# Other deadlines for two closing quarters of the last pair, and one reload split over two queues

## The chip, the cores and the metric

The kernel runs on one core of one Trainium2 chip. The metric is device time in microseconds (us): the median of three runs of the whole kernel. One further execution was taken with the hardware profiler. All durations below that belong to single instructions are from that one execution.

The engines are named as in the profile: PE is TensorE, DVE is VectorE, ACT is ScalarE, POOL is GpSimd, SP is SyncE. SP and ACT issue the DMA transfers of this kernel. Each of them works through its own list of instructions in order, so an issue that has to wait holds up everything behind it in that list.

## The reference

What is computed is one conditioned transformer-like block on `x` of shape (2, 2048, 512) in float32:

```python
emb = jnp.dot(jax.nn.silu(t), ada_w) + ada_b
shift_msa, scale_msa, gate_msa, shift_mlp, scale_mlp, gate_mlp = jnp.split(emb, 6, axis=-1)
norm = _ln(x) * (1.0 + scale_msa[:, None]) + shift_msa[:, None]
h = jax.nn.gelu(jnp.dot(norm, ssm_w1) + ssm_b1, approximate=False)
ssm_out = jnp.dot(h, ssm_w2) + ssm_b2
x = x + gate_msa[:, None] * ssm_out
norm2 = _ln(x) * (1.0 + scale_mlp[:, None]) + shift_mlp[:, None]
hf = jax.nn.gelu(jnp.dot(norm2, ff_w1) + ff_b1, approximate=True)
ff_out = jnp.dot(hf, ff_w2) + ff_b2
x = x + gate_mlp[:, None] * ff_out
```

Both weights of the first half are 512 x 512, `ff_w1` is 512 x 1024 and `ff_w2` 1024 x 512. The change touches only the last line, for the last tokens.

## The kernel before

**Tiling.** The 4096 tokens are cut into 8 blocks of 512. The first half of the function runs block by block. The second half, the feed-forward, runs on pairs of blocks: `ff` goes through four pairs, s = 0 to 3, first `up(s)`, then `down(s)`. "The last pair" is s = 3, and `closing` or `last` in the code means this pair.

**Fewer products.** All matrix products are done by a two-level scheme that replaces eight block products by seven, with sums of operands before and sums of results after. `down(s)` has seven outer products in the order P1, P2, P3, P6, P5, P7, P4 (`DOWN`, L939), and each of them seven inner ones, called leaves, in the order P1, P5, P6, P2, P7, P3, P4 (`CARRIED`, L447). Two outer products run interleaved: a leaf of one, then a leaf of the next. A leaf leaves its result in a PSUM bank, and DVE or ACT carries it into `summed`, four rows of results `r0` to `r3` in the tile `rows`. Operand sums run on DVE or POOL, as the planner decides.

**The quarters of a pair's result.** The result of a pair has four quarters: block 0 or 1 (`blk`) by the left or right half of the features (`d`). It stands with features on the partitions and tokens along them and has to be turned before it is added to the residual `x1`.

- In the last pair the two quarters with d = 0 go through DRAM, by `quarter_out` (L1065). The first, `blk` 0, is complete after outer product P2 (row `r0`); the second, `blk` 1, after outer product P5 (row `r3`). `quarter_out` transposes 32 x 32 blocks by two DVE instructions (L1073) into a band of the tile `far`, stores the four slices of the band to a DRAM buffer (`back`) on SP and ACT in turn, loads the buffer back into the same row (`rows<-back`, one load of 512 KB on SP), adds it in two halves (h = 0, 1) to the residual, and stores each half to the output, the first from SP and the second from ACT. The residual of the first quarter stands in the tile `far`, that of the second in `near`. So `out_dram<-far` are the first quarter's closing stores and `out_dram<-near` the second's.
- The two quarters with d = 1 are scaled and summed by DVE (`scaled_add`, L1045), then turned by PE with an identity matrix (`turned_by_pe`, L1183, matmuls on line 306), added to the residual in the tile `hidden` and stored in eight pieces of 128 KB, `out_dram<-hidden`. The turn of a leaf is put into PE's list two leaves later. Outer product P7 feeds one of these quarters by wide adds (128 x 512), P4 the other by narrow ones (128 x 256). P5 feeds `r3` by narrow scaled adds. The text below calls the add that follows a turn a `hidden` add.

**What sets the order.** The order of work on every engine is laid out when the program is built. Each operation is entered into `Plan` with an assumed cost. `order` (L89) gives each matmul a due time, at which it would start if PE ran without a gap, t being the end of that; it gives each closing store the due time t + 3000 ns (L101). From these it counts back a latest start (`late`) for every operation:

```python
late = min(late, ops[s].late - (1 + op.care) * (self.HOP + min(op.lat.values()) + op.size / self.RATE))
```

HOP is 70 ns and RATE 370 bytes per ns; `care` is 0.45 for all of the feed-forward (L1381 sets it last). The assumed latency is 2000 ns for a DMA, n/0.96 + 155 ns for a DVE add of n columns, n/0.96 + 205 for a scaled add, and 705 for a transpose. `simulate` (L113) then plays the program. On each engine it takes, of the operations that are ready, the one with the smallest `late` (`rank`, L141); it waits for one that is not ready only if that one is due to start before the ready one would end, has a smaller `late` than it, and can begin at least 150 ns before that end. PE's list keeps the order of the program. The result is a fixed list for each engine, which the chip works through in order.

Of the kernel before, what the change touches and what calls it, by code (L numbers as in the profile page):

```python
# [20 lines left out]
class Plan:  # L21
# [67 lines left out]
    def order(self):  # L89
        ops = self.ops  # L90
        for op in ops:
            if op.engs == "p":
                op.deps = {d for d in op.deps if ops[d].engs != "p"}
            for d in op.deps:
                ops[d].succ.append(op.n)
        t, due = 0.0, {}
        for op in ops:
            if op.engs == "p":
                due[op.n] = t
                t += op.cost["p"]  # L100
        due.update((n, t + 3000.0) for n in self.closing)  # L101
        for _ in range(2):
            for op in reversed(ops):
                late = due.get(op.n, 1e9)
                for s in op.succ:
                    late = min(late, ops[s].late - (1 + op.care) * (self.HOP + min(op.lat.values()) + op.size / self.RATE))
                op.late = late - op.sooner
            self.simulate()
            wait = ops[self.anchor].start - due[self.anchor]
            due = {n: t + wait for n, t in due.items()}  # L110
        return sorted(ops, key=lambda op: (op.start, op.n))
# [89 lines left out]
def kernel(  # L201
# [28 lines left out]
    M = P // G  # L230
# [6 lines left out]
    plan = Plan(nc)  # L237
# [6 lines left out]
    def cols(ap):  # L244
        n = 1
        for d in ap.shape[1:]:
            n *= d
        return n
# [4 lines left out]
    def tt(e, o, a, b, f):  # L253
        n, ps = cols(o), in_psum(a, b)
        cost = {"v": n / 0.96 + 70, "g": 2.12 * n + 145}
        plan.add(
            e,
            lambda E: E.tensor_tensor(o, a, b, f),  # L258
            [o],
            [a, b],  # L260
            cost,
            {"v": cost["v"] + 85, "g": cost["g"] + 45},
            "g" if ps else "vg",
        )
# [5 lines left out]
    def act(o, a, func, bias=0.0, scale=1.0):  # L270
        n = cols(o)
        ptrs = [p for p in (bias, scale) if not isinstance(p, float)]
        cost = n / 1.4 + (155, 215, 340)[len(ptrs)] + (30 if func == AF.Gelu_apprx_tanh else 0)
        plan.add(
            "a",
            lambda E: E.activation(o, a, func, bias=bias, scale=scale),  # L276
            [o],
            [a] + ptrs,
            {"a": cost},
            {"a": cost + 90},  # L280
        )
# [21 lines left out]
    def turn_by_pe(o, a, identity, start, stop):  # L303
        plan.add(
            "p",
            lambda E: E.matmul(o, a, identity, start=start, stop=stop, is_transpose=True, skip_group_check=True),  # L306
            [o],
            [a, identity],
            {"p": 120.0},
            {"p": 290.0},  # L310
        )

    def dma(o, a, q="s", lead=0.0, lat=2000.0, sooner=0.0):
        size = max(cols(o.unsqueeze(0)), 1) * 4
        outs = [o] if o.tensor.name in scratch else []
        ins = [a] if a.tensor.name in scratch else []
        lead = lead or (0.0 if ins or not outs or size <= plan.LITTLE else 25000.0)
        plan.add(q, lambda E: E.dma_start(out=o, in_=a), outs, ins, {q: plan.ISSUE}, {q: lat}, size=size, lead=lead)
        plan.ops[-1].sooner = sooner
# [24 lines left out]
    def kb(t, at, n):  # L344
        return t[:, at * 256 : (at + n) * 256]

    def cut(t, form, **sizes):
        return t.rearrange(form, **sizes)
# [6 lines left out]
    for n in range(8):  # L355
        t = psum.tile([P, 2 * HT], F32, tag=f"bank{n}", name=f"bank{n}")
# [699 lines left out]
    def columns(s, d, e, blk):  # L1056
        k, b = 2 * d + e, (2 * s + blk) // PER_B
        return gb5[:, k, b : b + 1], mods[5][:, k, b : b + 1]

    def rest_in(s, d, blk, x):  # L1060
        half = slice(d * D // 2, (d + 1) * D // 2)
        dma(x, x1_d[2 * s + blk][:, :, half])
        return x, out_blk[2 * s + blk][:, :, half]

    def quarter_out(s, d, blk, r, scaled=False):  # L1065
        done = summed[:, r]
        n = quarters[0] % 2
        for e in range(0 if scaled else 2):
            act(done[:, e], done[:, e], AF.Identity, *columns(s, d, e, blk))
        band = cut(bands[n], "p (a c e r) -> p e c a r", a=M, c=C, e=2)  # L1070
        for e in range(2):
            o, a = band[:, e], cut(done[:, e], "p (c a q) -> p c a q", c=C, a=M)
            plan.add("v", lambda E, o=o, a=a: E.transpose(o, a), [o], [a], {"v": 636}, {"v": 705})  # L1073
        closing = s + 1 == NBLK // 2
        queue = lambda f: "sa"[f % 2] if closing else "s"
        far_t = back_d[s][d][blk]
        for f in range(M):
            dma(far_t[:, f].rearrange("(a q) r -> q a r", a=M), cut(bands[n][f * G : (f + 1) * G], "p (a r) -> p a r", a=M), queue(f))
        flat = done.rearrange("p e t -> p (e t)")
        dma(flat, far_t.rearrange("p f r -> p (f r)"))  # L1080
        x, to = rest_in(s, d, blk, rest[n])
        for h in range(2):
            c = slice(2 * h, 2 * h + 2)
            o = cut(x[:, c], "p c (e f r) -> p (c e) f r", e=2, f=M)
            a = cut(flat, "p (f c e r) -> p c e f r", f=M, c=C, e=2)[:, c].rearrange("p c e f r -> p (c e) f r")
            tt("v" if closing else "vg", o, a, o, ALU.add)
            if closing:
                dma(to[:, c], x[:, c], queue(h))
                plan.closing.append(plan.ops[-1].n)
        if not closing:  # L1090
            dma(to, x)
        quarters[0] += 1

    def down(s):
# [22 lines left out]
        def leaf(n, f):  # L1117
# [23 lines left out]
            elif p == "P2":  # L1141
                add(r0, r1 if new else r0)
                if f == "P4":
                    quarter_out(s, 0, 0, 0)
# [5 lines left out]
            elif p == "P5":  # L1150
                if last:
                    scaled_add(r3, t, columns(s, 0, e, 1)[1])
                add(r2, r1 if new else r2)
                if full and last:
                    act(part[:, 1:3], part[:, 1:3], AF.Identity, *columns(s, 1, e, 0))
                elif full:
                    tt("vg", r3, r3, r2, ALU.add)
                if f == "P4":
                    quarter_out(s, 0, 1, 3, last)
            elif p == "P7":  # L1160
                both, wide = part[:, 1:3], t.unsqueeze(1).to_broadcast([P, 2, HT])
                if last:
                    scaled_add(both, wide, columns(s, 1, e, 0)[1])
                else:
                    tt("v", both, wide, both, ALU.add)
                if last:
                    turned_by_pe(1, 2, f, quad)
                elif f == "P4":
                    quarter_out(s, 1, 1, 2)
            elif not last:  # L1170
                add(r1, r1)
                if f == "P4":
                    quarter_out(s, 1, 0, 1)
            else:
                scaled_add(r1, t, columns(s, 1, e, 0)[1])
                turned_by_pe(0, 1, f, quad)
# [6 lines left out]
    def turned_by_pe(blk, r, f, quad):  # L1183
        got = tail[blk]
        if not got:
            got["x"], got["out"] = rest_in(NBLK // 2 - 1, 1, blk, cut(kb(hidden_r, 8 * blk, 4), "p (c d) -> p c d", c=C))

        def turned_back():
            e, h = int(quad[0]) - 1, int(quad[1]) - 1
            bank = cut(banks[TURNED_AT[blk][h]], "p (c e d) -> p c e d", c=2, e=2)  # L1190
            for c in range(2):
                col = slice((2 * h + c) * P, (2 * h + c + 1) * P)
                turn_by_pe(bank[:, c, e], summed[:, r, e, col], ident, c == 0 and h not in got, c == 1)
            got[h] = True
            c, d = slice(2 * h, 2 * h + 2), slice(e * P, (e + 1) * P)
            x = got["x"][:, c, d]
            tt("v", x, bank[:, :, e], x, ALU.add)
            dma(got["out"][:, c, d], x, "sa"[e])
            plan.closing.append(plan.ops[-1].n)

        n = leaves_read[0] = leaves_read[0] + 1
        if f in ("P7", "P2", "P3", "P4"):
            waiting.append((n, turned_back))
        done = blk == 0 and f == "P4"
        while waiting and (done or waiting[0][0] + 2 <= n):
            waiting.pop(0)[1]()
# [240 lines left out]
```

## Time and profile before

| | us |
|---|---|
| median of three runs (lowest, highest) | 564.51 (564.48, 564.86) |
| the profiled execution | 564.89 |
| its span, first to last instruction | 563.1 |
| PE busy in the span | 552.2 (98%) |
| DVE busy in the span | 479.8 (85%) |
| POOL busy in the span | 384.7 (68%) |
| ACT busy in the span | 282.6 (50%) |

The span is 1.8 us shorter than the profiled execution's time; these lie outside its first and last instruction. The profiled execution was 0.38 us longer than the median.

How to read the lines below. In the chain that ended last, a line is start, length, and what held up the end during it. In the order of time, a line is start, length from first to last instruction of the line, engine, source line, operation, what it writes and reads, the shape, how many instructions are merged, and in brackets the idle time just before it with what ended it. Lengths of neighbours on one engine can overlap a little. `SPq` and `ACTq` are the lists that issue DMA; such a line shows when the issue happened, not when the data moved. In the table by stretches, each engine has its busy time and the count of instructions, and the last three numbers are the granted PE clock, the mean busy share of the 16 DMA engines, and GB/s moved. A line of waits is who waited on whom, total us, times, and the longest.

### The profile page before, as it was taken

To read this page: it belongs to the slowest core of one execution; us is meant where nothing else is said; L and a number is where in the kernel's file an instruction comes from. 1 tells how busy PE (TensorE), PEld (TensorE's weight loads), DVE (VectorE), ACT (ScalarE), POOL (GpSimd) and SP (SyncE) were. 2 spreads that over 40 slices of the span, in tenths; PEclk is the share of its full clock that TensorE was granted. 3 is DMA by queue.
4 is the path that set the end of the run, shared out by engine and by line. 5 is a ranking of instruction groups with operands and counts; after the bars stand their busy time and mean duration, and the time that the engine had idled before them with its cause. 6 is when DMAs were issued, how large, how long until landed. Compare 5 with 4: busy or idle time off the path is not lost.

```text
span 563.1 us, 8745 instructions
## 1 busy us (share of the span) xinstructions
PE 552.2 (98%) x2809; PEld 481.2 (85%) x2809; DVE 479.8 (85%) x848; ACT 282.6 (50%) x523; POOL 384.7 (68%) x475
## 2 busy tenths in 40 slices
PE   7999999999999999999999999999999999999994
PEld 4888889888898988888878888888888888888883
DVE  5696878888778588899999996799988989998986
ACT  3473867674877855566205337414337315345230
POOL 2887747979945399984746778676767666547590
PEclk9999999999999999999999999999999999999998
DMA  8963899989399978994202899602998603974317
GB/s 310 399 228 79 234 349 312 330 258 274 100 288 318 303 289 257 334 281 166 75 2 50 286 331 313 210 17 63 306 321 298 183 33 104 309 252 154 108 38 224
DMA packets 66034, 123.68 MB, mean 220 GB/s; under 512 B 5653, under 2 KB 33221, under 8 KB 64453
## 3 DMA queue, kind: packets, MB, share of 16 engines
q1 hardware_dynamic: 63696, 121.53, 66.0%
q10 hardware_dynamic: 2292, 1.60, 1.0%
q8 instruction: 22, 0.36, 0.3%
q14 instruction: 24, 0.19, 0.1%
HBM read 77.89 MB, written 44.18 MB: 217 GB/s over the span
## 4 chain that ended last, share of the span: by engine, by line
PE 89%; DVE 6%; DMA 3%; issue 0%; POOL 0%; DVEq 0%; SPq 0%; ACTq 0%; POOLq 0%
PE bank L296 88%; DVE rows L258 2%; DMA fw<-in_L_cond_ada_w_dram 1%; DVE near L258 1%; DVE far L258 1%; DMA rows<-back 1%; DVE fw L258 1%; DMA back<-far 1%; PE bank L306 0%; DMA fw<-in_L_cond_ada_b_dram 0%; DVE far L1073 0%; DVE hidden L258 0%; POOL far L258 0%; POOL fw L258 0%; POOL rows L258 0%
## 5 line engine op out<-in xcount | busy, mean ns | idle before, releaser
L296 PE MATMUL bank<-turned,ring 128*128 128x256 f32 x896 | 210.2, 380 | 0.2 <-DVE turned L660 0.2
L296 PEld LDWEIGHTS bank<-turned,ring 128*128 128x128 f32 x896 | 167.9, 190 | 23.2 <-DVE turned L660 0.4
L258 DVE TENSOR_TENSOR hidden<-bank,hidden 128x512 f32<-128x512 f32 (+2 forms) x178 | 126.5, 740 | 23.4 <-PE bank L296 19.6
L296 PE MATMUL bank<-near,hidden 128*128 128x256 f32 (+1 forms) x470 | 95.1, 350 | 0.0
L296 PEld LDWEIGHTS bank<-near,hidden 128*128 128x128 f32 x470 | 82.2, 190 | 9.4 <-POOL near L258 0.3
L296 PE MATMUL bank<-far,fw 128*128 128x256 f32 (+1 forms) x354 | 86.0, 374 | 0.2
L258 POOL TENSOR_TENSOR turned<-turned 128x512 f32<-128x512 f32 (+1 forms) x62 | 70.4, 1146 | 20.6 <-DVE turned L258 9.1
L296 PE MATMUL bank<-ring 128*128 128x256 f32 x336 | 82.4, 379 | 0.0
L258 DVE TENSOR_TENSOR rows<-bank,rows 128x256 f32<-128x256 f32 (+1 forms) x142 | 66.2, 479 | 15.4 <-PE bank L296 11.4
L296 PEld LDWEIGHTS bank<-far,fw 128*128 128x128 f32 x354 | 66.5, 190 | 9.6 <-issue 0.5
L296 PEld LDWEIGHTS bank<-ring 128*128 128x128 f32 x336 | 63.7, 190 | 9.1 <-issue 0.5
L285 ACT COPY bank<-bank 128x512 f32<-128x512 f32 (+2 forms) x84 | 37.7, 449 | 62.1 <-PE bank L296 55.8
L276 ACT ACTIVATE hidden<-hidden,cols 128x512 f32<-128x512 f32 (+1 forms) x66 | 44.8, 710 | 43.0 <-DVE hidden L258 42.9
L258 POOL TENSOR_TENSOR hidden<-hidden 128x128 f32<-128x128 f32 (+2 forms) x45 | 43.5, 976 | 25.8 <-DVE hidden L258 13.0
L296 PE MATMUL bank<-near,fw 128*128 128x256 f32 (+1 forms) x246 | 60.7, 377 | 0.0
L296 PE MATMUL bank<-hidden,fw 128*128 128x256 f32 (+1 forms) x216 | 53.3, 376 | 0.5 <-DVE rows L258 0.4
L296 PEld LDWEIGHTS bank<-near,fw 128*128 128x128 f32 x246 | 46.1, 190 | 6.4 <-DVE rows L258 0.2
L276 ACT ACTIVATE turned<-turned,mod,mod 128x512 f32<-128x512 f32 x56 | 42.3, 807 | 9.2 <-DMA turned<-turned 8.5
L296 PEld LDWEIGHTS bank<-hidden,fw 128*128 128x128 f32 x216 | 40.3, 190 | 6.5 <-DVE rows L258 0.8
L276 ACT ACTIVATE rows<-rows,gb,mod 128x512 f32<-128x512 f32 (+1 forms) x34 | 26.7, 787 | 36.9 <-DVE rows L258 25.0
L258 POOL TENSOR_TENSOR ring<-turned,ring 128x256 f32<-128x256 f32 x42 | 30.6, 740 | 20.7 <-PE bank L296 17.0
L258 POOL TENSOR_TENSOR fw<-fw 128x256 f32<-128x256 f32 (+1 forms) x38 | 35.5, 945 | 11.4 <-DMA fw_parts<-fw 3.9
(123 smaller groups left out, 735.4 us busy)
## 6 DMA issues: line engine op xcount, KB each, us to landing
ring<-fw_parts SPq DMA_DIRECT2D x28, 512.0 KB, 5.0
turned<-far SPq DMA_DIRECT2D x52, 256.0 KB, 4.4
ring<-fw_parts SPq DMA_DIRECT2D x28, 384.0 KB, 5.4
turned<-turned SPq DMA_DIRECT2D x32, 256.0 KB, 5.6
rows<-back SPq DMA_DIRECT2D x14, 512.0 KB, 5.5
back<-far SPq DMA_DIRECT2D x52, 128.0 KB, 3.0
fw_parts<-fw SPq DMA_DIRECT2D x21, 256.0 KB, 4.8
fw<-in_L_cond_ada_w_dram SPq DMA_DIRECT2D x5, 1024.0 KB
```

Source lines behind the costliest of these rows:

```text
L258: lambda E: E.tensor_tensor(o, a, b, f),
L276: lambda E: E.activation(o, a, func, bias=bias, scale=scale),
L285: plan.add("a", lambda E: E.copy(o, a), [o], [a], {"a": cost}, {"a": cost + 60})
L296: lambda E: E.matmul(o, lhsT, rhs, start=start, stop=stop, skip_group_check=True, **kw),
```

## The change

The list of closing stores now holds a due time for each store. Before, each was due at t + 3000 ns. After, the first quarter's two closing stores are due at t - 4000, the second quarter's at t - 1000, and the eight stores of the turned quarters at t + 3000 as before. And for the second quarter alone, the reload of 512 KB on SP becomes two of 256 KB, the first on SP and the second on ACT. Each brings the columns that one of the two adds needs: in each of the four slots of 256 columns, the first or the last 128.

```diff
-        due.update((n, t + 3000.0) for n in self.closing)
+        due.update((n, t + late) for n, late in self.closing)
...
         flat = done.rearrange("p e t -> p (e t)")
-        dma(flat, far_t.rearrange("p f r -> p (f r)"))
+        by_slots = lambda t, h: cut(t, "p (f h r) -> p h f r", f=M, h=2)[:, h]
+        for h in range(2 if closing and blk else 0):
+            dma(by_slots(flat, h), far_t.rearrange("p f (h r) -> p h f r", h=2)[:, h], queue(h))
+        if not closing or not blk:
+            dma(flat, far_t.rearrange("p f r -> p (f r)"))
...
                 dma(to[:, c], x[:, c], queue(h))
-                plan.closing.append(plan.ops[-1].n)
+                plan.closing.append((plan.ops[-1].n, -1000.0 if blk else -4000.0))
...
             dma(got["out"][:, c, d], x, "sa"[e])
-            plan.closing.append(plan.ops[-1].n)
+            plan.closing.append((plan.ops[-1].n, 3000.0))
```

## The prediction

> **What bounds the kernel now.** I read the chain of work that ended last first, then the order of time of each queue and engine in the last 20 us, then the DMA share by stretches.
>
> ```profile
> 461.13 85.76 PE bank L296 x396
> ...
> 547.59 0.70 DVE far L1073
> ...
> 548.72 3.63 DMA back<-far
> 552.36 0.67 DVE far L258
> ...
> 553.64 4.22 DMA rows<-back
> ...
> 557.88 0.69 DVE near L258
> 558.57 0.60 DVEq L1442
> ```
>
> TensorE sets the time up to 546.9 us, unbroken since 461.13. From there the end is one thing: the second quarter of the last pair (blk 1, rows `r3`), which is transposed, stored to DRAM, loaded back, added and stored. The kernel loses 16 us between TensorE's release and the span's end at 563.1. The change touches only this tail, so its worth is read there.
>
> ```profile
> 548.32 0.78 SPq L318 DMA_DIRECT2D back<-far  x2
> 549.15 0.72 SPq L318 DMA_DIRECT2D out_dram<-hidden  x1
> 553.05 0.40 SPq L318 DMA_DIRECT2D out_dram<-far  x1
> 553.64 0.34 SPq L318 DMA_DIRECT2D rows<-back  x1
> ...
> 558.60 0.37 SPq L318 DMA_DIRECT2D out_dram<-near  x1
> ```
> ```profile
> 554.05 0.40 ACTq L318 DMA_DIRECT2D out_dram<-far  x1
> ...
> 559.20 0.38 ACTq L318 DMA_DIRECT2D out_dram<-near  x1
> ```
> ```profile
> SPq L318 <- DVE rows L1049: 4.0, 2, 3.5
> ```
>
> The last rows are SP's queue, ACT's queue, and SP's waits between 549 and 553.2. SP stands 3.5 us in one wait, on VectorE, ahead of the first quarter's store (`out_dram<-far`); the load `rows<-back` is queued behind it. The first quarter was loaded back long before (534.07, below): only its add was late.
>
> ```profile
> 542.94 3.00 DVE L1049 SCALAR_TENSOR_TENSOR rows<-bank,mod,rows 128x256 f32<-128x256 f32 x5
> 545.86 0.70 DVE L1073 STREAM_TRANSPOSE far<-rows 128x512 f32<-128x512 f32 x1
> 546.92 0.75 DVE L1049 SCALAR_TENSOR_TENSOR rows<-bank,mod,rows 128x512 f32<-128x512 f32 x1 [0.36 <-PE bank L296]
> 547.59 0.70 DVE L1073 STREAM_TRANSPOSE far<-rows 128x512 f32<-128x512 f32 x1
> ...
> 548.52 0.41 DVE L258 TENSOR_TENSOR hidden<-bank,hidden 128x256 f32<-128x256 f32 x1
> 548.86 0.75 DVE L1049 SCALAR_TENSOR_TENSOR rows<-bank,mod,rows 128x512 f32<-128x512 f32 x1
> 549.53 0.41 DVE L258 TENSOR_TENSOR hidden<-bank,hidden 128x256 f32<-128x256 f32 x1
> ...
> 552.34 0.68 DVE L258 TENSOR_TENSOR far<-rows,far 128x512 f32<-128x512 f32 x1
> 552.94 0.48 DVE L1049 SCALAR_TENSOR_TENSOR rows<-bank,mod,rows 128x256 f32<-128x256 f32 x1
> 553.33 0.68 DVE L258 TENSOR_TENSOR far<-rows,far 128x512 f32<-128x512 f32 x1
> 553.93 0.48 DVE L1049 SCALAR_TENSOR_TENSOR rows<-bank,mod,rows 128x256 f32<-128x256 f32 x1
> 554.33 0.75 DVE L258 TENSOR_TENSOR hidden<-bank,hidden 128x256 f32<-128x256 f32 x2
> ...
> 556.33 0.76 DVE L258 TENSOR_TENSOR hidden<-bank,hidden 128x256 f32<-128x256 f32 x2 [0.20 <-PE bank L306]
> 557.88 1.29 DVE L258 TENSOR_TENSOR near<-rows,near 128x512 f32<-128x512 f32 x2 [0.79 <-DMA rows<-back]
> ```
>
> This is VectorE in order of time. Starts follow each other more closely than durations say: 0.40 us for a narrow scaled add (553.93 to 554.33), 0.67 for a wide one (548.86 to 549.53), 0.62 for a transpose, 0.60 for a first-quarter add (`far`), 0.33 for a `hidden` add. The second transpose (547.59) stands behind a wide add that waited 0.36 us for TensorE. At the end VectorE waits 0.79 us for the load.
>
> ```profile
> 549.00:552.50 3.50, 3.50 (x19) 3.06 (x19) 3.12 (x7) 0.81 (x1) 0.63 (x1) 1.00 0.89 220
> 552.50:554.00 1.50, 1.50 (x11) 1.27 (x10) 1.50 (x4) 0.00 (x0) 0.00 (x0) 1.00 0.08 22
> 554.00:556.00 2.00, 1.30 (x8) 0.91 (x7) 2.00 (x7) 0.00 (x0) 0.00 (x0) 1.00 1.04 208
> 556.00:561.50 5.50, 0.51 (x4) 0.27 (x3) 2.18 (x5) 0.00 (x0) 0.00 (x0) 0.67 1.07 349
> ```
>
> The last two numbers are DMA share and GB/s. The engines idle from 552.5 to 554 and are then full from 556 to 561.5, moving 349 GB/s x 5.5 us = 1.92 MB. So the end is also a matter of bytes: the first quarter's stores (512 KB) and the load (512 KB), both held back, fall on top of the closing stores.
>
> **The ranks.** The planner lists each engine's operations by a rank, the latest start that still meets a deadline, counted back from the end of the matmuls t with 1.45 times its own costs (`care` 0.45). These are its numbers, not times of the chip; I use them only for order. A closing add stands 1.45 x 0.758 = 1.10 us before its store, so the first quarter's adds move from t+1.90 to t-5.10 and the second quarter's from t+1.90 to t-2.10. Back from there: a whole load 5.06, a half load 4.03, the stores 3.51, a transpose 1.12. The transposes go from t-7.80 to t-10.77. The wide add of 546.92 has t-8.03 (its turn on TensorE is due at t-6.86), the wide one before the first transpose, in the group of five, t-9.13. Old ranks reproduce the trace: -9.13, transpose, -8.03, transpose.
>
> **Part 1, the second quarter leaves earlier.** The two transposes now rank ahead of both wide adds. Nothing is added or removed. The group of five at 542.94 holds, by the view of its source line,
>
> ```profile
> L1049 DVE SCALAR_TENSOR_TENSOR rows<-bank,mod,rows x5: 476/744/751, 542.9 to 545.2; 128x512 f32<-128x512 f32 x3, 128x256 f32<-128x256 f32 x2
> ```
>
> three wide and two narrow; by the order of the leaves the last is wide. One narrow, two wide and one narrow remain ahead: 542.94 + 0.40 + 0.67 + 0.67 + 0.40 = 545.08, and two transposes of 0.62 end at 546.32, against 548.29. The four `back` stores then go at 546.35 instead of 548.32: **-1.97 us**. Late in return are the two wide adds: 546.32 and 546.99. Behind the first waits TensorE's turn:
>
> ```profile
> 547.37 0.35 PEld L306 LDWEIGHTS bank<-far,rows 128*128 128x128 f32 x2
> ```
>
> It ends at 547.07 and the weights load at 547.37, a cover of 0.30 us; if that goes, each further VectorE operation ahead costs 0.4 to 0.7 us on TensorE. I take nothing. Upstream, the accumulations and ACT operations into `r3` rank about 3 us earlier too and may trade places with operand sums on VectorE and GpSimd; TensorE had no gap there. I take 0, bounds -0.2 and +1.3 (two first-quarter adds' worth).
>
> **Part 2, the first quarter's adds move forward.** At t-5.10 they pass both early `hidden` adds (t+2.29) and three narrow or wide adds (t-4.58 to t-3.48), not those due earlier. In the places of 548.52 and 549.53 they run at about 548.0 and 549.53. The `out_dram<-far` stores leave SP at about 548.6 instead of 553.05 and ACT at about 550.2 instead of 554.05: 512 KB into a stretch before 552.5-554, where the share is 0.08. Two `hidden` adds of 0.33 go to the freed 1.20 us after 552.3. VectorE's total is unchanged; I take 0.15 us off the last `hidden` add (bounds 0 and 0.2, its own wait).
>
> **Part 3, the load.** The first quarter shows the interval from store to load on a free SP, and the page the median landing of all such loads:
>
> ```profile
> 530.19 0.80 SPq L318 DMA_DIRECT2D back<-far  x2
> 534.07 0.34 SPq L318 DMA_DIRECT2D rows<-back  x1
> ```
> ```profile
> rows<-back SPq DMA_DIRECT2D x14, 512.0 KB, 5.5
> ```
>
> 3.88 us, so at best 546.35 + 3.88 = 550.2. If a `hidden` store stands ahead on SP or ACT, the load waits for that add: after 550.13, two narrow and one wide add (1.47) and two `hidden` adds give 552.3. I take 552.3, nearest to how SP stands now. With 4.22 us (553.64 to 557.85) it lands at 556.5, before VectorE's last `hidden` add ends (557.09, now 556.95). The wait of 0.79 goes; late next is VectorE itself. Both halves cost one more issue (0.4 us, ACT free then) and moves runs an eighth as long (512 bytes, 4 KB before). The eight 128 KB `hidden` stores have such runs and share the stretch of 349 GB/s. Bounds for the split: -0.60 (the first add under the second half) and +1.3 (4.22 against the 5.5 us of the page's row below); both bounds count only past 556.95, until when VectorE covers the load, so I take 0. The Trainium skill ("DMA: Bandwidth & Descriptors", section "Issuing engines are not separate DMA queues") speaks against the split: transfers started by two engines share the same 16 DMA engines and interleave, and only issue time is saved. By that rule the halves land together and the split is worth 0 even when the load is late; no run here shows it yet.
>
> **Sum.** The last store leaves at 559.20 - 0.79 - 0.15 = 558.26: -0.94. It took 3.9 us to land. The 128 KB `back` stores of the first quarter took
>
> ```profile
> DMA to landing us min/median/max: 2.7/2.7/2.7
> ```
>
> so 256 KB alone needs 2.7 + 128 KB / 349 GB/s = 3.1 us; 0.8 was queueing. From 556 on there remain 768 + 512 = 1280 KB instead of 1.92 MB, 1.8 us less of full DMA, which is enough to clear most of it. Between -0.94 (3.9 stays) and -1.74 (3.1) I take **-1.5**, since the bytes left bind less than the issue. Profiled execution: span 563.1, 564.89 us in all; 564.89 - 1.5 = 563.4. That run lies 0.38 above the median, so from the median 564.51: **563.0 us**. 0.2% is 1.13 us, about what a measurement of this kernel can tell from no change.
>
> **Rivals.**
> *VectorE only* (0.17). The wait goes, but the last store still lands in 3.9 us since `hidden` and `near` stores now follow each other more closely. For it: six of eight `hidden` stores are issued after 554.7. Against: 640 KB less after 556. 564.51 - 0.94 = 563.6.
> *The load stays late* (0.15). The loads are queued on SP and ACT behind `hidden` stores whose adds run after 553, or the ranks change little: landing at 557.5 or later. With both halves at 557.5, 1.29 us of adds end at 558.8: 564.1, and up to 564.5 if nothing moves. By the skill's rule above it is this; if the first half came 0.73 us (256 KB / 349 GB/s) earlier, it would be 563.5.
> *Slower* (0.08). The earlier ranks put transposes and first-quarter adds ahead of the scaled adds that TensorE's turns wait for. It decides as soon as over 0.30 us more stands ahead of the add ending at 547.07. Two first-quarter adds (1.20) and a transpose (0.62) there make 1.8 - 0.3 = 1.5 us stall; all of the tail follows, and the gain at the end, bound by TensorE then, is lost: 564.51 + 1.3 to 1.5 = 565.9.
>
> **How the numbers follow.** The forecast has 0.60 and is the case of faster (562.2 to 563.38); same is the next two, 0.17 and 0.15: 0.32; slower 0.08. The range reaches from 562.2 (-2.3: the load at 550.2 and the second quarter's adds ahead of the last `hidden` adds) to 564.7 (nothing moves, or a small stall).
>
> **What would show it.** Right: the transposes follow each other directly and the `back` stores go near 546.4; `out_dram<-far` leaves SP before 550; two 256 KB loads issue by 552.5; no wait for DMA ahead of the `near` adds; the share in 552.5 to 554 rises and the full stretch after 556 ends before 560.5; span near 561.6. Wrong: a new TensorE wait on VectorE at the turns of 547 to 549, a gap in the matmuls between 461 and 547, a load still issued after 553, or last stores that take 3.9 us again.

## The result, and the profile after

| | before | after |
|---|---|---|
| median of nine runs (us) | 564.72 | 563.16 |
| lowest to highest | 564.48 to 565.1 | 563.06 to 563.47 |
| profiled execution, span | 564.89, 563.1 | 563.11, 561.3 |

The ratio after to before is 0.9973 with a 95% interval of 0.9963 to 0.9983: 1.56 us less. The profiled spans differ by 1.8 us. Of this 0.16 arose before the tail: the narrow add of VectorE that waits for TensorE before the group of five starts at 542.60 before and at 542.44 after. About 1.64 us come from the stretch that the change touches, the tail from this add to the end of the span: 20.5 us before, 18.9 after.

First SP's list, then ACT's, of the changed kernel in order of time. A line is start, length, and what is issued.

```profile
546.02 0.78 SPq L318 DMA_DIRECT2D back<-far  x2
548.63 0.41 SPq L318 DMA_DIRECT2D out_dram<-hidden  x1
550.41 0.40 SPq L318 DMA_DIRECT2D out_dram<-far  x1
550.98 0.53 SPq L318 DMA_DIRECT2D rows<-back  x1
...
557.56 0.37 SPq L318 DMA_DIRECT2D out_dram<-near  x1
```
```profile
551.01 0.40 ACTq L318 DMA_DIRECT2D out_dram<-far  x1
551.59 0.60 ACTq L318 DMA_DIRECT2D rows<-back  x1
...
558.16 0.38 ACTq L318 DMA_DIRECT2D out_dram<-near  x1
```

The `back` stores go 2.30 us sooner than at 548.32, the reload 2.66 us sooner on SP, the first quarter's first store 2.64 us sooner, and the last store 1.04 us sooner. From the last store to the end of the span it took 561.3 - 558.16 = 3.1 us, where it took 3.9.

VectorE of the changed kernel, in order of time:

```profile
543.29 0.71 DVE L1073 STREAM_TRANSPOSE far<-rows 128x512 f32<-128x512 f32 x1
544.23 1.14 DVE L1049 SCALAR_TENSOR_TENSOR rows<-bank,mod,rows 128x256 f32<-128x256 f32 x2 [0.23 <-PE bank L296]
545.29 0.70 DVE L1073 STREAM_TRANSPOSE far<-rows 128x512 f32<-128x512 f32 x1
545.92 2.03 DVE L1049 SCALAR_TENSOR_TENSOR rows<-bank,mod,rows 128x512 f32<-128x512 f32 x3
...
549.37 0.41 DVE L258 TENSOR_TENSOR hidden<-bank,hidden 128x256 f32<-128x256 f32 x1
549.70 1.28 DVE L258 TENSOR_TENSOR far<-rows,far 128x512 f32<-128x512 f32 x2
...
556.18 0.76 DVE L258 TENSOR_TENSOR hidden<-bank,hidden 128x256 f32<-128x256 f32 x2 [0.53 <-PE bank L306]
556.85 1.28 DVE L258 TENSOR_TENSOR near<-rows,near 128x512 f32<-128x512 f32 x2
```

The last line has no wait in brackets: the 0.79 us for the load are gone, and the `near` adds follow the last `hidden` adds without a gap. What VectorE waits for now is TensorE's last turns (0.53 us, where it was 0.20). The chain that ended last says the same. It held two DMA steps from 548.72 to the `near` adds, and now has none behind 460.98: it follows TensorE without a gap to 554.81, and then VectorE and TensorE in turn.

```profile
554.83 0.48 DVE rows L1049
555.31 0.34 DVE hidden L258
555.66 0.04 issue
555.70 0.45 PE bank L306 x2
556.15 0.02 issue
556.18 0.42 DVE hidden L258
556.60 0.33 DVEq L1446
556.93 1.20 DVE near L258 x2
```

The stretches with DMA share and GB/s at the end of each line:

```profile
552.50:554.00 1.50, 1.50 (x11) 1.32 (x10) 1.50 (x5) 0.00 (x0) 0.00 (x0) 1.00 0.97 220
554.00:556.00 2.00, 1.31 (x9) 0.95 (x8) 1.41 (x4) 0.00 (x0) 0.00 (x0) 1.00 1.16 337
556.00:561.50 5.50, 0.36 (x4) 0.12 (x2) 1.95 (x4) 0.00 (x0) 0.00 (x0) 0.79 0.58 182
```

The hole from 552.5 to 554 (share 0.08) is filled, and after 556 there remain 182 GB/s x 5.5 us = 1.0 MB instead of 1.92.

### The profile page after: what moved, and what is told of

Its sections match the earlier page's. It is cut to its first block, busy times and chain, and to the rows that moved or that the text cites. A ratio compares the mean times of both kernels' runs of the same rounds, so it can differ in the third digit from the quotient of the medians.

```text
span 561.3 us, 8747 instructions
## 1 busy us (share of the span) xinstructions
PE 552.9 (98%) x2809; PEld 481.7 (86%) x2809; DVE 479.2 (85%) x848; ACT 282.9 (50%) x523; POOL 385.0 (69%) x475
## 4 chain that ended last, share of the span: by engine, by line
PE 91%; DVE 6%; DMA 2%; POOL 0%; issue 0%; DVEq 0%; POOLq 0%
PE bank L296 90%; DVE rows L258 2%; DVE near L258 1%; DMA fw<-in_L_cond_ada_w_dram 1%; DVE far L258 1%; PE bank L306 1%; DVE fw L258 1%; DVE hidden L258 0%; DMA fw<-in_L_cond_ada_b_dram 0%; DVE far L1073 0%; POOL far L258 0%; POOL fw L258 0%; POOL rows L258 0%; DVE turned L660 0%; DVE rows L1049 0%
## 5 line engine op out<-in xcount | busy, mean ns | idle before, releaser
L258 POOL TENSOR_TENSOR turned<-turned 128x512 f32<-128x512 f32 (+1 forms) x62 | 70.4, 1148 | 20.4 <-DVE turned L258 9.0
```

## The experiments

All times are medians, and each is compared with the kernel before as it ran beside it on the same chip. Theory A is the prediction's: a wait for the load and a queue of bytes, both ended by what leaves early. Theory B: the split earns the gain, because its halves land sooner. Theory C: the earlier transposes earn it. The others came up on the way. The ratio is worked out from the runs, not from the two medians, so it need not equal their quotient.

| run | us | before | difference | ratio (95%) |
|---|---|---|---|---|
| split only | 564.53 | 564.94 | -0.41 | 0.9992 (0.9984 to 1.0001) |
| first quarter's deadline only | 563.30 | 564.94 | -1.64 | 0.9974 (0.9965 to 0.9983) |
| second quarter's deadline only | 563.52 | 564.94 | -1.42 | 0.9974 (0.9964 to 0.9984) |
| both deadlines, no split | 563.92 | 564.94 | -1.02 | 0.9983 (0.9974 to 0.9992) |
| one load, same rank | 563.45 | 564.90 | -1.45 | 0.9972 (0.9962 to 0.9983) |
| two loads, early rank | 564.36 | 564.90 | -0.54 | 0.9991 (0.9982 to 1.0000) |
| one late store more | 563.88 | 564.90 | -1.02 | 0.9986 (0.9977 to 0.9995) |
| near adds between hidden adds | 563.07 | 564.90 | -1.83 | 0.9965 (0.9953 to 0.9978) |
| the changed kernel again | 563.19 | 564.81 | -1.62 | 0.9969 (0.9958 to 0.9981) |
| first quarter's deadline only, again | 563.37 | 564.81 | -1.44 | 0.9975 (0.9965 to 0.9985) |
| near adds between, again | 563.36 | 564.81 | -1.45 | 0.9973 (0.9963 to 0.9984) |
| reload before the far store | 562.93 | 564.81 | -1.88 | 0.9964 (0.9952 to 0.9977) |

The profiles give a second reading, free of what arose ahead of the tail: the tail in us, from the narrow add of VectorE that waits 0.76 to 0.78 us for TensorE to the end of the span. Where a kernel has two profiles, both are given.

| kernel | add starts | span | tail |
|---|---|---|---|
| before | 542.60 | 563.1 | 20.5 |
| changed | 542.44, 542.52 | 561.3, 561.4 | 18.9, 18.9 |
| split only | 543.29 | 563.7 | 20.4 |
| first quarter's deadline only | 542.28, 542.53 | 562.0, 562.3 | 19.7, 19.8 |
| second quarter's deadline only | 543.00 | 562.2 | 19.2 |
| both deadlines, no split | 543.17 | 562.7 | 19.5 |
| one load, same rank | 542.99 | 561.9 | 18.9 |
| two loads, early rank | 542.50 | 562.2 | 19.7 |
| one late store more | 542.54 | 562.0 | 19.5 |
| near adds between hidden adds | 542.62, 542.77 | 561.4, 561.6 | 18.8, 18.8 |
| reload before the far store | 542.61 | 561.2 | 18.6 |

The tails lose what the medians lose to within 0.35 us, except for the first quarter's deadline alone, of which more below.

**1. The parts alone.** The split alone (against the changed kernel):

```diff
-                plan.closing.append((plan.ops[-1].n, -1000.0 if blk else -4000.0))
+                plan.closing.append((plan.ops[-1].n, 3000.0))
```

> Only the reload in two halves; all deadlines as before. The first of the two out_dram<-far stores still stands ahead of the first half on SP, the second ahead of the second half on ACT. Theory A (the prediction's: the gain is the wait for the load, 0.8 to 0.95 us, plus the queue under the last stores, 0.6 to 0.8, and both come from what leaves early; the split is worth nothing): -0.2 to -0.6 us, only what the altered order of the adds happens to bring. Theory B (the split earns it, its halves land earlier): -1.2 us or more. Theory C (the earlier transposes of the second quarter earn it): 0.

It gave -0.41 us, with 1 in its interval. Its profile (its slowest execution) shows why two queues did not help. SP's and ACT's lists:

```profile
553.55 0.53 SPq L318 DMA_DIRECT2D rows<-back  x1
```
```profile
553.79 0.41 ACTq L318 DMA_DIRECT2D out_dram<-far  x1
554.37 0.62 ACTq L318 DMA_DIRECT2D rows<-back  x1
```

and VectorE:

```profile
559.22 1.29 DVE L258 TENSOR_TENSOR near<-rows,near 128x512 f32<-128x512 f32 x2 [1.50 <-DMA rows<-back]
```

The half on SP left when the `back` stores had landed, for which SP waited 0.9 us; its `out_dram<-far` store had gone at 552.13. The half on ACT stands behind the other late `out_dram<-far` store. It left at 554.37 and the `near` adds waited until 559.22, 4.85 us later, for 256 KB; before, 512 KB took 4.22. Part of the delay in this execution came earlier: its `back` stores went at 549.46 instead of 548.32. Theory B falls for this kernel: without the deadlines the second queue only moves the wait.

The first quarter's deadline alone:

```diff
+                plan.closing.append((plan.ops[-1].n, 3000.0 if blk else -4000.0))
...
+        for h in range(0):
...
+        if True:
```

> Only the first quarter's deadline (t-4000); second quarter at t+3000, one reload. Theory A: the out_dram<-far stores leave near 550.5, SP is free when the back stores have landed (about 552.3), the load lands near 556.5, so most of the gain is here: -1.2 to -1.5 us. Theory B: under -0.5. Theory C: under -0.5, since the transposes stay at 545.9 and 547.6.

-1.64 us, and -1.44 in the second series, by the medians about as much as the whole change (-1.56 and -1.62). Theory C falls as the only cause, since the transposes stay where they were (545.54 and 547.27 in its profile). In that profile SP reads:

```profile
550.26 0.75 SPq L318 DMA_DIRECT2D out_dram<-far  x1
552.25 0.34 SPq L318 DMA_DIRECT2D rows<-back  x1
```

The store no longer holds the load; what holds it is the landing of the `back` stores. But the load did not land near 556.5, as expected: it took 5.16 us in one profile and 5.19 in the other, where it had taken 4.22. Both profiled executions of this kernel still waited for it, 0.65 and 0.69 us, and both lie above its median (563.79 and 564.06 us against 563.30 and 563.37), with tails that are only 0.8 and 0.7 us shorter than before. An execution at the median, without a profile, would then have waited little or not at all; that is inferred, not seen. Its runs spread more, from 563.20 to 565.25 and from 563.19 to 564.06; those of the changed kernel lie from 563.06 to 563.47 and from 563.15 to 563.27. So the other two parts give little to the median and, as far as the spread and these two profiles show, take away an exposure. How often the load comes late without them was not measured apart, and why it took longer to land stays open.

The second quarter's deadline alone:

```diff
+                plan.closing.append((plan.ops[-1].n, -1000.0 if blk else 3000.0))
...
+        for h in range(0):
...
+        if True:
```

> Only the second quarter's deadline (t-1000); first quarter at t+3000, one reload, which now stands ahead of the first out_dram<-far store on SP, and the near adds stand ahead of the last two hidden adds on VectorE. Theory A: load near 550, landed near 554.5, so the near adds fill VectorE's wait for the last turns and the last stores are 128 KB ones: -1.4 to -2.0 us, if the load is there by 555.4; each us that it is later costs one. Theory B: 0 to -0.5. Theory C: -1.2 to -1.6.

-1.42 us, by another road: on SP the reload passes the first quarter's store (550.35 and 552.09), and on VectorE the `near` adds pass the last two `hidden` adds. No add waits for the load. This run fits theory C as well as A; it is the run before that tells them apart. The gains of the two deadlines do not add up, which fits their ending the same wait.

Both deadlines without the split:

```diff
+        for h in range(0):
...
+        if True:
```

> Both deadlines as in the changed kernel, but one reload of 512 KB on SP as before. Theory A: the split is covered, so as the changed kernel, -1.4 to -1.6 us against before. Theory B: -0.5 or less. Theory C: -1.4 to -1.6.

-1.02 us, less than either deadline alone by the medians, though the intervals overlap. Theory A had expected the changed kernel's time. The trace shows a wait of TensorE that neither the kernel before nor the changed one has, but that the second quarter's deadline alone has too (at 546.81). Here it is with VectorE around it:

```profile
546.98 1.10 PE L296 MATMUL bank<-hidden,fw 128*128 128x256 f32 x4 [0.39 <-DVE rows L1049]
```
```profile
544.02 0.71 DVE L1073 STREAM_TRANSPOSE far<-rows 128x512 f32<-128x512 f32 x1
544.97 0.48 DVE L1049 SCALAR_TENSOR_TENSOR rows<-bank,mod,rows 128x256 f32<-128x256 f32 x1 [0.23 <-PE bank L296]
545.49 0.71 DVE L1073 STREAM_TRANSPOSE far<-rows 128x512 f32<-128x512 f32 x1
546.12 2.75 DVE L1049 SCALAR_TENSOR_TENSOR rows<-bank,mod,rows 128x512 f32<-128x512 f32 x4
```

Four wide adds stand behind the second transpose, where the changed kernel has three. That gave theory D: the split matters through the rank. A whole load counts 5.06 us in the planner's arithmetic and a half load 4.03, so with one load the transposes rank at t-11.80 instead of t-10.77, pass one wide add too many, and TensorE waits for a bank that this add has not yet emptied. It costs more than the 0.39 us in brackets, since a matmul's start follows the one before more closely than durations say: from the second group ahead of the wait (544.70) to the next turn (548.78) TensorE takes 4.08 us, and from the same group to the same turn in the changed kernel (543.96 to 547.41) 3.45. The 0.63 us are about what the median lacks (-1.02 against -1.56 and -1.62).

**2. The rank, with the transfer held fixed, and the reverse.** One load with the rank of two:

```diff
-                plan.closing.append((plan.ops[-1].n, -1000.0 if blk else -4000.0))
+                plan.closing.append((plan.ops[-1].n, 30.0 if blk else -4000.0))
...
+        for h in range(0):
...
+        if True:
```

> Both deadlines, one reload of 512 KB on SP, but the second quarter due at t+30 instead of t-1000, so that its transposes have the changed kernel's rank (t-10.77). All lists of all engines are then those of the changed kernel but for the load itself. Theory D (the split is worth something only by the rank: a whole load counts 5.06 where a half counts 4.03, which put the second transpose ahead of one wide add too many and made TensorE wait 0.39 us): as the changed kernel, -1.4 to -1.7 us, no such wait. Theory B (the split brings the data sooner): as the kernel with both deadlines and one load, -1.0.

-1.45 us, against -1.02 with the earlier rank, and no wait of TensorE at that place. As transfers, one load and two halves differ by 0.1 to 0.2 us by the medians (-1.45 against -1.56 and -1.62), inside the intervals, and by less than 0.1 us in the tail (18.9 us each). Two loads with the rank of one:

```diff
-                plan.closing.append((plan.ops[-1].n, -1000.0 if blk else -4000.0))
+                plan.closing.append((plan.ops[-1].n, -2030.0 if blk else -4000.0))
```

> The changed kernel with the second quarter due at t-2030, so that its transposes have the rank they had with one load (t-11.80). Theory D: TensorE waits 0.39 us for a wide add near 546.8 again although the load is split. By that alone 0.4 us slower than the changed kernel, -1.0 to -1.2 against before; the two near adds move between the last hidden adds, which can give back 0.3 to 0.6. Theory B: no wait, at least as fast as the changed kernel.

-0.54 us, less than the -1.0 to -1.2 expected. The wait is back although the load is split:

```profile
546.31 1.10 PE L296 MATMUL bank<-hidden,fw 128*128 128x256 f32 x4 [0.39 <-DVE rows L1049]
```

So theory D holds in both directions for the wait. TensorE again takes 4.08 us to the next turn. The rest of this kernel's loss, beyond what was expected, lies at its end, where the order differs too: its first `near` add waited 0.16 us for the load, its last turns waited for VectorE 1.55 us instead of 0.69, and its last store was a `hidden` one on ACT; this was not taken apart further.

**3. The queue of bytes.** One store of 512 KB more, of the finished first quarter, to a scratch buffer:

```diff
+        if closing and not blk:
+            dma(far("extra", P, C, D // 2), x, "s", lead=2500.0)
+            plan.closing.append((plan.ops[-1].n, 3000.0))
```

> The changed kernel with one store more: the finished first quarter, 512 KB, to a scratch buffer in DRAM, issued on SP between the second and third of its last hidden stores. It puts back as many bytes as the change took out of the end. Theory A (the last store's landing is a queue of bytes): the near adds stay where they are, the last store lands 0.5 to 1.0 us later, -0.5 to -1.1 against before. Rival (its landing of 3.1 to 3.9 us has nothing to do with the bytes): -1.4 to -1.6, as the changed kernel.

-1.02 us against before, so 0.5 to 0.6 us of the gain are given back. SP and then ACT of its profile:

```profile
555.15 0.49 SPq L318 DMA_DIRECT2D extra<-far  x1
```
```profile
558.28 0.38 ACTq L318 DMA_DIRECT2D out_dram<-near  x1
```

The last store leaves as in the changed kernel (558.16, and 558.25 in its second profile) but the span ends at 562.0, 3.7 us later instead of 3.1. At its end SP waits for `out_dram<-near` (2.8 us), and nothing waits for the extra store. The bytes queued set the landing: theory A's second term stands, and the rival falls. 512 KB cost no more than this because part of them fills DMA time that is idle in the changed kernel: the share from 556 to 557 and from 557 to 558 rises from 0.68 and 0.51 to 1.16 and 0.95.

**4. The wait that binds the changed kernel.** The planner's `care` is lowered for the two reloads, so that it reckons them to land sooner (its ranks count the transposes back by 0.42 us less, too, and the `back` stores go at 546.73 instead of 546.11):

```diff
+            plan.care = 0.3
             dma(by_slots(flat, h), far_t.rearrange("p f (h r) -> p h f r", h=2)[:, h], queue(h))
+            plan.care = 0.45
```

> The changed kernel with care 0.3 instead of 0.45 for the two reloads, so that the planner reckons them to land sooner; on VectorE the near adds then stand between the last three hidden adds, and both transposes follow each other behind one wide add. What binds the changed kernel's end is VectorE: it waits 0.53 us for the last turns and then does two hidden and two near adds. Theory E (this wait can be filled if the halves are there by 555.6): -0.4 to -0.8 us against the changed kernel, -2.0 to -2.4 against before. Rival (the halves land after 555.6 and VectorE stands in front of them): 0 to +0.5 against the changed kernel.

> The kernel with the near adds between the last hidden adds, again: 0.2 to 0.4 us faster than the changed kernel beside it, as the first run of it showed; if that was chance, within 0.15 us.

-1.83 us in one series, short of the -2.0 to -2.4 expected, and -1.45 in the next, 0.17 us slower than the changed kernel beside it. So it is not to be told from the changed kernel; the lead of the first series did not come again. The order on VectorE is as wanted, but the load is the limit again, as the rival said; the chain of the second profile:

```profile
551.93 4.23 DMA rows<-back
556.16 0.02 issue
556.19 0.69 DVE near L258
```

The half on ACT stands behind a store there and arrives just too late. So with the first quarter due at t-2500 besides, which puts that half ahead of the store:

```diff
-                plan.closing.append((plan.ops[-1].n, -1000.0 if blk else -4000.0))
+                plan.closing.append((plan.ops[-1].n, -1000.0 if blk else -2500.0))
```

> The same, with the first quarter due at t-2500 instead of t-4000: its second add moves behind three scaled adds, and on ACT the second half's reload stands ahead of the second out_dram<-far store. If what holds the near adds there is the reload (it landed at 555.92, just ahead of the first near add), the second half lands 0.3 to 0.6 us sooner; the order on VectorE gives the near adds nothing before 555.8, so -0.1 to -0.3 against the kernel before it. Rival: 256 KB more of closing stores fall into the end, +0.2 to +0.5.

```profile
555.74 0.68 DVE L258 TENSOR_TENSOR near<-rows,near 128x512 f32<-128x512 f32 x1
556.35 0.42 DVE L258 TENSOR_TENSOR hidden<-bank,hidden 128x256 f32<-128x256 f32 x1
556.70 0.68 DVE L258 TENSOR_TENSOR near<-rows,near 128x512 f32<-128x512 f32 x1
557.29 0.42 DVE L258 TENSOR_TENSOR hidden<-bank,hidden 128x256 f32<-128x256 f32 x1
```

No add waits for the load, and VectorE is done at 557.7 instead of 558.1. The median is 562.93 us, 0.26 below the changed kernel beside it; the runs do not overlap (562.87 to 563.00, and 563.15 to 563.27). Against the kernel with the `near` adds between it is 0.43 below, more than the 0.1 to 0.3 expected. The rival named there holds in part: the last store leaves at 557.74, 0.5 us sooner than the changed kernel's in the same series, but takes 3.5 us instead of 3.1 to the end of the span. This is the fastest version of the study. The difference is small beside what one comparison can settle. The two repeats:

> The changed kernel itself, beside the next three on one chip: -1.5 to -1.7 us.

> Only the first quarter's deadline, again. If the second quarter's deadline and the split add nothing of their own, within 0.2 us of the changed kernel. If the wait of 0.65 us for the reload that its profile showed is the rule and not a chance, 0.4 to 0.7 us slower than the changed kernel.

The first came out at -1.62, inside its expectation. The second was 0.18 us slower than the changed kernel by the median, inside the 0.2 us of its first case, though its profile waits for the load as the first one did.

## Why the prediction held, and where its steps were off

**Part 1, the transposes: right, by the ranks.** The `back` stores were put at 546.35 and went at 546.02. The worked order was two transposes in a row behind two wide adds; in fact they stand apart (543.29 and 545.29), and the second lies behind one wide add only. Of the 0.33 us 0.16 arose ahead of the tail; the rest is the wide add that is missing (0.67), less a wait of 0.23 for TensorE between the transposes and less closely packed starts. The price that part 1 named for going further, TensorE waiting for a displaced wide add, did not fall due in the changed kernel but did in three variants (0.39 us in brackets and 0.63 by the starts, in each). The rival *slower* was thus the right mechanism with the wrong place: it binds first at the bank of a leaf at 546.3 to 547.0, not at the turn at 547.37, and the margin was one wide add. At the turn the cover of 0.30 us did go, as feared: the weights load waits 0.16 us for VectorE there in the changed kernel, but the matmuls behind it start without a gap.

**Part 2, the first quarter's adds: right that they move, wrong by 1.7 us where.** "In the places of 548.52 and 549.53 they run at about 548.0 and 549.53" failed: both stand at 549.70, behind the `hidden` adds they should have passed. The reason, read from the planner's code and not tested apart, is not the rank but a lock: the planner does not start an add with both inputs in SBUF on VectorE while GpSimd is in one, and GpSimd's last sum in the changed kernel is

```profile
548.18 1.28 POOL L258 TENSOR_TENSOR far<-near,far 128x512 f32<-128x512 f32 x1
```

which ends at 549.46. The variant with both deadlines and no split shows what this guards against. The plan's times are not the chip's, and there one such add came up at 549.51, beside GpSimd's sum from 548.92 to 550.19:

```profile
548.92 1.27 POOL L258 TENSOR_TENSOR far<-near,far 128x512 f32<-128x512 f32 x1
```
```profile
549.51 1.24 DVE L258 TENSOR_TENSOR far<-rows,far 128x512 f32<-128x512 f32 x1
```

It took 1.24 us instead of 0.68. The two loads with the early rank show the same: 1.24 us from 548.84, beside a sum that ended at 549.53. The Trainium skill ("SBUF — State Buffer", section "Who interferes with whom") says that a VectorE instruction with two SBUF inputs contends with a GpSimd instruction that reads SBUF, that what they contend for is an exclusive lock, and that the order of issue decides who blocks. If the later one blocks until the other ends, the add would end one add after 550.19, at 550.87; it ended at 550.75, so the trace agrees to 0.12 us. The slip cost the forecast nothing, since the stores still left 2.64 us earlier and found the DMA engines nearly idle (a share of 0.15 from 550.0 to 550.5).

**Part 3, the load: right that it is covered, only half right on what is late next.** Issue was put at 552.3 and came at 550.98 and 551.59, and no add waits for the load. "Late next is VectorE itself" holds from 554.83 on; ahead of that the chain runs along TensorE, and VectorE waits for it. The split was taken at 0 as a transfer, and experiment 2 agrees. What the prediction did not see is that the split changes the rank by 1.03 us and that 0.4 to 0.6 us hang on it; it took the half load's rank for granted and never asked what the whole load's would do. The rule of the Trainium skill that transfers started by two engines share the same DMA engines ("DMA: Bandwidth & Descriptors", section "Issuing engines are not separate DMA queues") fits the halves: 4.23 us from issue to landing for 256 KB in the chain of experiment 4, and 4.22 for 512 KB before. What else was queued differs between the two, and no run here shows when each half landed.

**The sum.** The last store was to leave at 558.26 and left at 558.16, 1.04 us sooner instead of 0.94; 0.16 of this arose ahead of the tail, so 0.88 are the change's. Two terms behind it were off, and it was luck that they nearly cancelled. The wait for the load was taken at 0.79, the time in brackets; by the starts it was worth 0.88 (from the last two `hidden` adds to the `near` adds 1.55 us before, 0.67 after). The 0.15 us off the last `hidden` adds did not come from the change: they start at 556.18 instead of 556.33, no more than the whole tail is early, since they follow TensorE. The landing was to shrink from 3.9 towards 3.1 us, of which the forecast took 0.56 of the 0.8, and it took 3.1. The bytes left after 556 were 1.0 MB, fewer than the 1280 KB reckoned. Nearly all of the lower bound of -1.74 came true in the tail (-1.64), and 1.56 of it in the medians.

## What to carry to other kernels

Look at what is queued behind a late and unimportant wait: here an add that nobody needed soon, ranked last, kept a store waiting, the store kept a load waiting on the same list, and the bytes of both fell into the end. In a planned schedule every edit has two effects, one on the chip and one on the plan's ranks; to find which of them earned the gain, hold one fixed and move the other, as with one load at the rank of two. Deadlines that end the same wait do not add up, and drawn too early they cost what they push aside.

## What was not expected of the hardware

A landing time is not a property of the transfer: the same 256 KB store took 3.9 us (before), 3.7 (one late store more) and 3.1 (changed) from issue to the end of the span, and the more bytes were still queued, the longer. And one execution's profile can sit above its kernel's median: the split alone was profiled at 565.54 us with a median of 564.53, so its wait of 1.50 us for the load is that of one execution and not of the median.
